# Two VectorE instructions of a graph dilation are tied to their place in the program

## The chip, the cores and the metric

The kernel runs on one NeuronCore of a Trainium2 chip. A core has TensorE (matmuls, here called PE), VectorE (DVE), ScalarE (ACT), GpSimd (POOL) and SyncE (SP, which here only issues transfers). The metric is the device time of one execution in microseconds; the figure given for a kernel is the median of its runs.

## The reference

Two graph layers follow each other on 16 graphs of 1024 nodes with 128 features each, in float32. Each layer normalises x, applies a relu, runs three convolutions and adds its result to x.

Layer 0 is, three times over for each graph:

```
h   = h @ W + b
nh  = h / |h|
ew  = adj * (nh @ nh.T)      # cosine of every pair of nodes times the edge
h   = ew @ h                 # relu after the first two
```

Layer 1 first thins out each graph's adjacency, which is the *dilation*. It goes through the rows one after the other, and each row's removals also clear the column:

```
row  = carry[n]; num = sum(row); sf = (num + 1) // 2 if num > 10 else 1
rank = cumsum(row)
rm   = row & (rank % sf == 0)          # if the node is valid and num > 1
carry[n] = row & ~rm;  carry[:, n] &= ~rm
```

Three graph convolutions with batch normalisation over all nodes follow on the thinned adjacency, then a projection. The result of the dilation depends on adj alone, so it can be worked out while layer 0 runs.

## The kernel before, in words

**Two strands.** The first part of the kernel interleaves layer 0 (the generator `layer0`) with the dilation (the generator `dilation`). The loop at the end of that part takes one step of the dilation, and then as many steps of layer 0 as bring both to the same share of their estimated work; the numbers that the generators yield are these estimates. This fixes only the order in which the program is written down.

**Who sets the order on an engine.** The program is written with a tile framework whose scheduler reorders each engine's instructions: it simulates the kernel and, among instructions whose inputs it takes as ready, issues first what was written first. So an instruction that is written late but ready early can be placed far ahead. `tc.keep_in_program_order(ins)` takes this freedom from one instruction: it puts an edge from the instruction that was written just before it on the same engine, so that it is issued behind that one. The edge concerns the order of issue alone; no semaphore is waited for. Two kinds of instructions of the dilation have such an edge before the change: the scans on VectorE (line 741) and the |rank - shift| on ScalarE (line 751).

**Layer 0.** The adjacency of a graph is brought in by blocks of 128 x 128. `adj_piece` (line 245) loads a block column into `nat` (two buffers), `adjT_tile` (line 253) loads the rows into `adjA`, and TensorE turns `nat` (line 260). For each block row, `products` multiplies the normalised features on TensorE into `pg` (line 344, two PSUM buffers), and VectorE multiplies `pg` with the adjacency into `ew` (lines 353 and 356). `turn` transposes ew (lines 373 and 374), and `sums` and `sums_back` add up ew @ h in PSUM (lines 384 and 398). Here as everywhere, an engine works through its queue in the order in which it was placed.

**The dilation.** Rows are treated in 8 blocks of 128, and each block in two halves of 8 graphs, which makes 16 half blocks. Each has three phases:

- *loads*, for each of the 8 graphs: the rows of adj come into `an` (line 585, two buffers). ScalarE turns the part from the diagonal on into a 0/1 pattern (lines 587 and 588: Sign, then Relu with a row sum, `rest`). For the part left of the diagonal, the columns removed by earlier blocks come through a transposing DMA from DRAM into `kl` (line 591, two buffers), and VectorE makes the pattern and its row sum `left` in one instruction, **line 594**. After every fourth graph, the diagonal blocks are turned and multiplied on TensorE (608 to 616) into the distances `T` (618), with `rbias` from VectorE (611).
- *rounds*: an iteration over the 128 rows of the block that finds which of them remove which diagonal entries (`Z`, `E`, `x`; lines 625 to 722).
- *scans*, for each of the 8 graphs: VectorE runs the cumulative sum over 1024 columns, `rank` (line 741). One graph later ScalarE takes |rank - shift| (line 751), and VectorE compares it with `radius`, **line 762**, which gives `kp`: 1 where an edge stays. GpSimd stores it to DRAM (line 763).

The loads of the next half block are written one by one between the scans of the present one: scan, layer-0 steps, load, layer-0 steps, comparison of the graph before, layer-0 steps, next scan. The patterns live in a ring of 10 slots, 8 for one half block and 2 ahead.

**After the dilation.** A flag tells whether an exact version has to run (a branch at line 824, not taken for these inputs). Layer 0 then ends, and layer 1 follows; none of it is edited.

Of the kernel before, what the change touches and what calls it, by code (L numbers as in the profile page):

```python
# [12 lines left out]
ALU = mybir.AluOpType  # L13
# [3 lines left out]
P = 128  # L17
# [29 lines left out]
def tile_adj_preln_d2(  # L47
# [40 lines left out]
    nc = tc.nc  # L88
# [111 lines left out]
    with ExitStack() as actx:  # L200
# [18 lines left out]
        for fill, value, op in ((0.0, -2.0, ALU.is_ge), (4.0 * FAR, 2.0 * FAR, ALU.is_gt)):  # L219
# [4 lines left out]
                up, up, pattern=[[1, P]], compare_op=op, fill=fill, base=0, channel_multiplier=-1  # L224
# [338 lines left out]
        def dilate(k, half, exact):  # L563
# [6 lines left out]
            def pattern(i):  # L570
                return patt[:, (at0 + i) % SLOTS, :]

            left = poold.tile([P, BH], F32, tag="left", name=f"left{nk}")
# [7 lines left out]
            def loads():  # L581
                for i in range(BH):
                    b = half * BH + i
                    an = poold.tile([P, N], F32, tag="an", name=f"an{nk}_{i}")
                    nc.sync.dma_start(an, adj[b, cols, :])
                    on = pattern(i)[:, 2 + k * P :]
                    nc.scalar.activation(on, an[:, k * P :], AF.Sign)
                    nc.scalar.activation(on, on, AF.Relu, accum_out=rest[:, i : i + 1])
                    if k:
                        pk = poold.tile([P, NCH - 1, P], F16, tag="kl", name=f"kl{nk}_{i}")  # L590
                        nc.sync.dma_start(
                            pk[:, :k, :].rearrange("p j q -> p (j q)"), keep_d[b][: k * P, cols], transpose=True
                        )
                        nc.vector.scalar_tensor_tensor(
                            pattern(i)[:, 2 : 2 + k * P],
                            an[:, : k * P],
                            0.0,
                            pk[:, :k, :].rearrange("p j q -> p (j q)"),
                            ALU.is_gt,
                            ALU.mult,  # L600
                            accum_out=left[:, i : i + 1],
                        )
                    if i % GT == GT - 1:
                        four = range(i - GT + 1, i + 1)
                        bs_ = slice(i - GT + 1, i + 1)
                        pdt = ps_sm.tile([P, GT, P], F16, tag="sm", name=f"pdt{nk}_{i}")
                        for n, ii in enumerate(four):
                            nc.tensor.transpose(pdt[:, n, :], pattern(ii)[:, diag], ident16)
                        dT = poold.tile([P, GT, P], F16, tag="dT", bufs=1, name=f"dT{nk}_{i}")
                        nc.scalar.activation(dT, pdt, AF.Copy)  # L610
                        nc.vector.tensor_scalar(rbias[:, bs_], rest[:, bs_], 2.0, -2.0, ALU.mult, ALU.add)
                        pT = ps_sm.tile([P, GT, P], F32, tag="sm", name=f"pT{nk}_{i}")
                        for n, ii in enumerate(four):
                            nc.tensor.matmul(pT[:, n, :], lhsT=dT[:, n, :], rhs=upto, start=True, stop=False)
                            nc.tensor.matmul(pT[:, n, :], lhsT=pattern(ii)[:, diag], rhs=off, start=False, stop=False)
                            nc.tensor.matmul(pT[:, n, :], lhsT=ident16, rhs=after, start=False, stop=True)
                        for n, ii in enumerate(four):
                            nc.scalar.activation(T[:, ii, :], pT[:, n, :], AF.Identity, bias=rbias[:, ii : ii + 1])
                    yield 0.8
# [105 lines left out]
            def scans():  # L725

                i = 0
                while i < BH:
                    at_ = (at0 + i) % SLOTS
                    n = min(BH - i, SLOTS - at_)  # L730
                    here = patt[:, at_ : at_ + n, diag]
                    nc.vector.tensor_tensor(here, here, E[:, i : i + n, :], ALU.subtract)
                    i += n
                ranks = {}
                for i in range(BH + 1):
                    if i < BH:

                        pt = pattern(i)
                        ranks[i] = rank = poold.tile([P, N], F16, tag="rank", bufs=3, name=f"rank{nk}_{i}")
                        tc.keep_in_program_order(  # L740
                            nc.vector.tensor_tensor_scan(rank, pt[:, 1 : N + 1], pt[:, 2:], 0.0, ALU.add, ALU.add)  # L741
                        )
                        yield True, 2.5
                    if i == 0:
                        continue

                    i -= 1
                    b = half * BH + i
                    pt, rank = pattern(i), ranks.pop(i)
                    tc.keep_in_program_order(  # L750
                        nc.scalar.activation(  # L751
                            rank, rank, AF.Abs, bias=shift[:, i : i + 1], scale=1.0 if exact else -1.0
                        )
                    )
                    kp = poold.tile([P, N], F16, tag="kp", name=f"kp{nk}_{i}")
                    if exact:
                        nc.vector.tensor_scalar(
                            kp, rank, low[:, i : i + 1], radius[:, i : i + 1], ALU.max, ALU.not_equal
                        )
                        nc.vector.tensor_tensor(kp, kp, pt[:, 2:], ALU.is_ge)  # L760
                    else:
                        nc.vector.tensor_scalar(kp, rank, radius[:, i : i + 1], None, ALU.not_equal)
                    nc.gpsimd.dma_start(keep_d[b][cols, :], kp)
                    yield False, 0.8

            return loads(), rounds(), scans()

        units0 = layer0()
# [448 lines left out]
```

## Time and profile before

| | |
|---|---|
| median of 3 runs | 2819.08 us (2816.39 to 2822.73) |
| the profiled execution | 2820.68 us |
| its span, first to last instruction | 2818.8 us |
| PE busy in the span | 2649.9 us, 94% |
| DVE busy | 1947.1 us, 69% |
| ACT busy | 1426.5 us, 51% |
| POOL busy | 477.6 us, 17% |
| scans, line 741 | 128, 2305 ns each |
| comparisons, line 762 | 128, 547 ns each |
| patterns left of the diagonal, line 594 | 112, 769 ns each |

The dilation lies in the first 1524 us of the span. In the waits of the profile, "PE pg L344 <- DVE ew L356" reads: the TensorE instruction of line 344 that writes pg waited for the VectorE instruction of line 356 that writes ew. Waits and idle times of an engine that is not the bound cost nothing by themselves. DVE_READ_ACCUMULATOR rows belong to the instruction ahead of them; it fetches a row sum.

### The profile page before, as it was taken

Reading aid. Unit: us, or ns where it says so; the run is one execution under the profiler, and the core shown is the slowest. Engines: PE = TensorE matmul, PEld = TensorE weight load, DVE = VectorE, ACT = ScalarE, POOL = GpSimd, SP = SyncE. Lnnn points to the kernel's source line nnn. Section 1 sums busy time; section 2 is a strip of 40 time slices with the busy share of each in tenths; the row PEclk is TensorE's granted clock in tenths of the full one; section 3 lists DMA queues with packets and bytes.
Section 4 is the critical chain, followed back from the end, with each engine's and each line's share of the span. In section 5 each row is a group of like instructions: output and inputs, shape, how many; then the busy total and the mean of one; then the engine's idle time right before and its main releaser. Section 6 shows DMA issues by size and latency. Waiting matters only on the chain. (4 is left out here: it accounts for less than half of the span.)

```text
span 2818.8 us, 51980 instructions
## 1 busy us (share of the span) xinstructions
PE 2649.9 (94%) x18803; PEld 2193.2 (78%) x18803; DVE 1947.1 (69%) x4943; ACT 1426.5 (51%) x4097; POOL 477.6 (17%) x616
## 2 busy tenths in 40 slices
PE   6999999999999999999999999999989999999997
PEld 4666666676776676666676778888889999899997
DVE  3778778788888788889886467777762333456556
ACT  6757667558556566466454333343333334333334
POOL 3112112012012111121121012222220101010101
PEclk9999999999999999999999999999999999999999
DMA  8437347258366476386354069999976666576774
GB/s 283 135 128 241 99 159 240 75 159 245 85 201 173 101 226 186 95 254 182 93 178 162 1 234 386 402 402 387 402 297 214 203 216 201 188 238 228 234 237 135
DMA packets 382233, 585.22 MB, mean 208 GB/s; under 512 B 85200, under 2 KB 266448, under 8 KB 381968
## 3 DMA queue, kind: packets, MB, share of 16 engines
q1 hardware_dynamic: 343280, 425.28, 48.2%
q0 software_dynamic: 38688, 156.53, 14.8%
q8 instruction: 151, 2.47, 0.4%
q14 instruction: 114, 0.93, 0.1%
HBM read 403.44 MB, written 163.58 MB: 201 GB/s over the span
## 5 line engine op out<-in xcount | busy, mean ns | idle before, releaser
L890 PE MATMUL agg<-hw,aT 128*128 128x128 f32 (+1 forms) x6144 | 743.5, 277 | 8.2 <-DVE aT L995 7.3
L890 PEld LDWEIGHTS agg<-hw,aT 128*128 128x128 f32 x6144 | 713.4, 193 | 13.6 <-DVE aT L995 9.7
L344 PE MATMUL pg<-nhT 128*128 128x512 f32 (+3 forms) x1152 | 454.7, 497 | 40.4 <-DVE ew L356 39.1
L384 PE MATMUL po<-ew,hS 128*128 128x512 f32 (+3 forms) x1152 | 453.3, 497 | 8.1 <-ACT hTo L407 3.7
L356 DVE TENSOR_TENSOR ew<-pg,adjA 128x768 f32<-128x768 f32 (+3 forms) x528 | 423.6, 826 | 5.0 <-PE pg L344 5.0
L398 PEld LDWEIGHTS po<-ew,hS 128*128 128x128 f32 x2688 | 339.5, 193 | 39.1 <-issue 36.8
L398 PE MATMUL po<-ew,hS 128*128 128x128 f32 x2688 | 367.5, 277 | 1.2 <-ACT ew L374 1.2
L374 ACT ACTIVATE ew<-gt 128x512 f32<-128x512 f32 (+1 forms) x480 | 208.5, 464 | 245.3 <-PE gt L373 238.0
L741 DVE TENSOR_TENSOR_SCAN rank<-patt 128x1024 f16<-128x1024 f16 x128 | 294.9, 2305 | 0.1
L344 PEld LDWEIGHTS pg<-nhT 128*128 128x128 f32 x1152 | 187.9, 192 | 131.7 <-issue 89.3
L384 PEld LDWEIGHTS po<-ew,hS 128*128 128x128 f32 x1152 | 195.2, 193 | 99.8 <-issue 64.6
L373 PEld LDWEIGHTS gt<-ident,ew 128*128 128x128 f32 x1344 | 168.5, 143 | 100.7 <-issue 75.4
L373 PE MATMUL gt<-ident,ew 128*128 128x128 f32 x1344 | 212.3, 277 | 4.8 <-PEq L824 2.5
L948 POOL TENSOR_TENSOR o<-o,rn 128x512 f32<-128x512 f32 x93 | 108.5, 1167 | 638.3 <-DVE rn L942 627.6
L353 DVE TENSOR_TENSOR ew<-pg,adjA 128x128 f32<-128x128 f32 x384 | 108.1, 282 | 156.6 <-PE pg L344 117.3
L864 DVE TENSOR_TENSOR own<-pw,bs 128x256 f32<-128x256 f32 x192 | 81.4, 424 | 155.5 <-ACT hw L863 155.4
L862 PE MATMUL pw<-wrx,hT 128*128 128x256 f32 x768 | 179.7, 388 | 9.2 <-ACT hT L1065 8.4
L862 PEld LDWEIGHTS pw<-wrx,hT 128*128 128x128 f32 x768 | 145.1, 194 | 31.3 <-ACT hT L1065 9.2
L1013 ACT ACTIVATE aT<-pta 128x512 f32<-128x512 f32 (+3 forms) x160 | 71.3, 467 | 187.4 <-PE pta L1012 181.9
L751 ACT ACTIVATE rank<-rank,fin 128x1024 f16<-128x1024 f16 x128 | 146.7, 1151 | 36.3 <-DVE rank L741 35.6
L940 ACT ACTIVATE own<-o 128x128 f32<-128x128 f32 x378 | 112.7, 301 | 99.7 <-DVE o L919 99.5
L321 POOL TENSOR_TENSOR hS<-hN,rn 128x1024 f32<-128x1024 f32 x48 | 102.5, 2136 | 355.5 <-DVE rn L157 226.0
(169 smaller groups left out, 3930.6 us busy)
## 6 DMA issues: line engine op xcount, KB each, us to landing
an<-in_adj_dram SPq DMA_DIRECT2D x128, 512.0 KB, 4.3
keep<-kp POOLq DMA_DIRECT2D x128, 256.0 KB, 2.9
kb<-keep SPq DMA_DIRECT2D x128, 256.0 KB, 5.5
aT<-adT SPq DMA_DIRECT2D x32, 960.0 KB, 4.7
aT<-adT SPq DMA_DIRECT2D x32, 832.0 KB, 4.6
aT<-adT SPq DMA_DIRECT2D x32, 704.0 KB, 4.2
aT<-adT SPq DMA_DIRECT2D x32, 576.0 KB, 3.4
xb<-in_x_dram SPq DMA_DIRECT2D x31, 512.0 KB, 5.2
```

Source lines behind the costliest of these rows:

```text
L344: nc.tensor.matmul(pg[:, :n, :].rearrange("p c q -> p (c q)"), lhsT=self.nhT[:, q * P : (q + 1) * P], rhs=self.nhT[:, (q + c) * P : (q + c ...
L356: nc.vector.tensor_tensor(both[0][:, :, off, :], pg[:, own:n, :].unsqueeze(1).to_broadcast([P, 2, n - own, P]), both[1][:, :, off, :], ALU ...
L373: nc.tensor.transpose(pt[:, i, :], ew[:, at + i, :], ident)
L374: nc.scalar.activation(ew[:, at : at + n, :], pt[:, :n, :], AF.Copy)
L384: nc.tensor.matmul(self.po[:, c * P : (c + n) * P], lhsT=self.hS[:, q, :], rhs=ew[:, c - q : c - q + n, :].rearrange("p c q -> p (c q)"), ...
L398: nc.tensor.matmul(self.po[:, q * P : (q + 1) * P], lhsT=self.hS[:, q + n, :], rhs=ew[:, NCH - 1 - q + n, :], start=False, stop=closes and ...
L741: nc.vector.tensor_tensor_scan(rank, pt[:, 1 : N + 1], pt[:, 2:], 0.0, ALU.add, ALU.add)
L751: nc.scalar.activation(rank, rank, AF.Abs, bias=shift[:, i : i + 1], scale=1.0 if exact else -1.0)
L862: nc.tensor.matmul(pw[:, i, :], lhsT=hT[:, 2 * h + i, :], rhs=wrx[:, l, :], start=True, stop=True)
L890: nc.tensor.matmul(self.place(c), lhsT=aT[:, blk, :], rhs=self.hw[:, source, :], start=source == 0 and c % self.ga == 0, stop=ends(c, source),
L940: nc.scalar.activation(sq, o, AF.Square, accum_out=ss[:, c : c + 1])
L948: nc.gpsimd.tensor_tensor(self.o[:, hc, :], self.o[:, hc, :], rn.unsqueeze(2).to_broadcast([P, CPH, D]), ALU.mult)
```

## The change

The instruction of line 594 (the pattern left of the diagonal) and that of line 762 (the comparison of the ranks) are each wrapped in `tc.keep_in_program_order`. What they compute is unchanged. The variant of the comparison that belongs to the exact version stays as it is. Lines behind the edits carry numbers that are up to two higher afterwards.

```diff
-                        nc.vector.scalar_tensor_tensor(
-                            pattern(i)[:, 2 : 2 + k * P],
-                            an[:, : k * P],
-                            0.0,
-                            pk[:, :k, :].rearrange("p j q -> p (j q)"),
-                            ALU.is_gt,
-                            ALU.mult,
-                            accum_out=left[:, i : i + 1],
+                        tc.keep_in_program_order(
+                            nc.vector.scalar_tensor_tensor(
+                                pattern(i)[:, 2 : 2 + k * P],
+                                an[:, : k * P],
+                                0.0,
+                                pk[:, :k, :].rearrange("p j q -> p (j q)"),
+                                ALU.is_gt,
+                                ALU.mult,
+                                accum_out=left[:, i : i + 1],
+                            )
                         )
...
                     else:
-                        nc.vector.tensor_scalar(kp, rank, radius[:, i : i + 1], None, ALU.not_equal)
+                        tc.keep_in_program_order(nc.vector.tensor_scalar(kp, rank, radius[:, i : i + 1], None, ALU.not_equal))
                     nc.gpsimd.dma_start(keep_d[b][cols, :], kp)
```

## The prediction

> **What bounds the kernel now.** I read the table of stretches first, then the waits of TensorE, then the timeline around the longest of them, then the waits of the DMA queue and the groups of the two edited lines. The branch of line 824 ends the only part in which the built programs differ: behind it every engine has the same instructions in the same order. So the stretch from 80 us (set-up) to 1524 us (branch) is the one to read; columns are start:end, length, then busy us and (count) by engine, TensorE clock, DMA share, GB/s.
>
> ```profile
> core 0: us, PE busy (x) PEld busy (x) DVE busy (x) ACT busy (x) POOL busy (x), PEclk, DMA share, GB/s
> 80.00:1524.00 1444.00, 1362.54 (x8627) 994.60 (x8626) 1194.50 (x2811) 896.55 (x2392) 251.94 (x314) 0.99 0.55 161
> ```
>
> TensorE is busy in 94% of it, VectorE in 83%. TensorE is the bound; VectorE matters only where TensorE waits for it. That is 1444 - 1362.5 = 81.5 us of idle TensorE at most, and these are its largest waits there:
>
> ```profile
> engine line waited for: us in total, times, longest us
> PE pg L344 <- DVE ew L356: 39.1, 37, 3.2
> PE pT L614 <- ACT dT L610: 5.5, 7, 1.4
> PE pw L293 <- ACT adjA L261: 4.2, 6, 0.9
> ```
>
> Half of the idle time is one wait: the cosine products pg have two PSUM buffers, and TensorE stands until VectorE has multiplied an older one into ew. What VectorE did instead is in the timeline before one such wait (start, length, engine, line; last a row of TensorE):
>
> ```profile
> 947.75 0.44 DVE L762 TENSOR_SCALAR kp<-rank,fin 128x1024 f16<-128x1024 f16 x1
> 948.10 2.29 DVE L741 TENSOR_TENSOR_SCAN rank<-patt 128x1024 f16<-128x1024 f16 x1
> 950.30 2.45 DVE L594 SCALAR_TENSOR_TENSOR patt<-an,kl 128x640 f16<-128x640 f32 x1
> ...
> 952.69 0.28 DVE L353 TENSOR_TENSOR ew<-pg,adjA 128x128 f32<-128x128 f32 x1
> 952.89 2.07 DVE L356 TENSOR_TENSOR ew<-pg,adjA 128x768 f32<-128x768 f32 x2
> ...
> 953.98 0.46 PE L344 MATMUL pg<-nhT 128*128 128x128 f32 x2 [2.86 <-DVE ew L356]
> ```
>
> A comparison, a scan and a pattern stand in one run of 4.9 us ahead of ew, and TensorE loses 2.86 us. Going through all 37 waits in this way, a pattern of line 594 lies in the run directly ahead in 22, which hold 26.6 of the 39.1 us.
>
> The two lines that are edited, as groups (busy us, mean ns | idle before them):
>
> ```profile
> L594 DVE SCALAR_TENSOR_TENSOR patt<-an,kl 128x128 f16<-128x128 f32 (+6 forms) x112 | 85.5, 769 | 6.8 <-DMA kl<-keep 5.9
> ...
> L762 DVE TENSOR_SCALAR kp<-rank,fin 128x1024 f16<-128x1024 f16 x128 | 69.2, 547 | 55.5 <-ACT rank L751 55.1
> ```
>
> VectorE idles 55.5 us in front of comparisons, since ScalarE's |rank - shift| is late, and hardly in front of patterns. The DMA queue's own waits:
>
> ```profile
> SPq L585 <- DVE patt L594: 397.9, 59, 48.6
> SPq L245 <- PE pt_a L260: 186.8, 81, 8.1
> ...
> SPq L253 <- DVE ew L356: 91.8, 42, 12.0
> ```
>
> The loads of adjacency rows (line 585) wait for the pattern two loads earlier to free their buffer.
>
> **What the Trainium skill says.** "PSUM — Partial Sum Buffer", section "Engine vs sequencer instructions": VectorE's and ScalarE's queues are strict first-in first-out. The trace agrees: ew at 952.69 follows the 2.45 us pattern. So an instruction queued too early costs what stands behind it. "Perfetto Trace Analysis", section "Identifying the Most-Contended Engine": improve that engine, and judge TensorE by LDWEIGHTS share rather than matmul share. That share here is 994.6/1444 = 69%, so busy TensorE may hide a little more than 81.5 us; I don't count on it. "SBUF — State Buffer", section "SBUF: two separate sides": VectorE and GpSimd lock a shared port pair for a whole instruction. The trace agrees: 8 patterns run over 0.2 us beyond their shape's median (2.45 against 0.82 us), and all 8 overlap a GpSimd multiply. The edit leaves such meetings to chance.
>
> **The change part by part.** Nothing is added or removed: both edits put an issue-order edge to the VectorE instruction traced just before, with no semaphore. What moves is where the scheduler places things, which the built orders show. Part of VectorE's queue in one half block (S scan, p pattern, k comparison, . the first ew product of a row):
>
> ```
> before  Sp..Sp..k.S.pk.S.p.kk.Sp..Sp..kSkSp..p..
> after   S.p.S.p.k.S.pk.S.p.k.S.pk.S.p.kS..pkS..p
> ```
>
> *Patterns.* All 112 move later, by 13.2 us of layer-0 VectorE work in the mean (24.5 us of the old trace's time in the median). They went in as soon as their data was expected; now one follows each scan, usually behind an ew row. Two estimates of the gain. Upper: take from each of the 22 waits the patterns ahead of it, min(wait, pattern): 20 us, or 20/86 = 0.23 us of TensorE per us of pattern. Lower: the patterns still run, and lengthen other runs. Adding up, at the trace's median durations, all that stands between ew products, what exceeds 3 us per run goes from 230 us to 195 us in the new order, 15% less, and runs above 4 us from 64 to 59; 15% of 39.1 us is 6 us. I take 9 us, nearer to the lower one because it counts what the patterns displace.
>
> *Comparisons.* Against layer-0 work, 88 of 128 stay within 0.5 us, 32 go later, 8 earlier, and of those with the largest waits (4.34, 3.88, 3.28, 3.10 us) none moves. They wait for ScalarE, whose |rank - shift| was pinned before. I cost this part at nothing, 0 to -3 us.
>
> *Loads.* Of each an the buffer is freed later, so an and kl fall 3.5 and 4.1 places back in the DMA queue among the layer-0 loads (one or two in the median), which go ahead; TensorE waits only 1.7 us for nat here, so little is gained. The kl loads (transposing, median 4.1 us to landing) ended 14.2 us ahead of their pattern in the median; placing the new order on the old trace's times leaves 12.5 us, 3.6 us at the least. So nothing waits; without that cover a pattern waiting for kl holds ew behind it, at 0.23 us of TensorE per us.
>
> *ScalarE.* Sign and Relu of the diagonal's right side (587, 588) move 2.8 us of ScalarE work later. They stood 93.5 us in ScalarE's queue waiting for a scan to free a pattern slot, with the transposed ew copies behind them. Part of that falls away; TensorE's waits on ScalarE are some 16 us, so I take -1 us (0 to -3). The later Relu leaves the diagonal transposes (608) about 10 of their 20 us, and rbias (611), 8.9 us later, at least 3.0 us before ScalarE needs it (before: 9.5 at the least from the second block on).
>
> *TensorE, GpSimd.* Of 5035 layer-0 TensorE rows 211 shift by over three places; keep stores move by at most two GpSimd places. Nothing.
>
> Sum: -9 - 0 - 1 - 0 = -10 us on a span of 2818.8 us, plus the 1.9 us around it: 2810.7 us, against 2820.68 us for the profiled execution. That one lay 1.6 us above the median of 2819.08 us, so the median becomes 2809 us.
>
> **The rivals.** *No measurable change, 2816 us.* The patterns only pass their delay to other ew rows, and waits on the scans (2.3 us each, most of every run) remain; about 3 us is left. For it: 15 of the 37 waits have no pattern ahead. Against it: the runs above 3 us do shrink. *A larger gain, 2797 us.* The upper estimate holds (20 us), with 2 us by ScalarE. For it: the new order has one pattern per scan, so that two patterns or scan plus pattern seldom meet. Against it: "pk" and "pkS" runs are new. *Slower, 2827 us.* The two-deep rings of an and kl lose their lead: a pattern, no longer early, finds kl not landed, as in three cases now (5.9 us, one of 2.87 us). At 0.23 us of TensorE per us, it takes (10 + 5.6)/0.23 = 68 us of VectorE waits at patterns, 0.6 us for each, to become measurably slower; 80 us of them give 18 - 10 = +8 us. For it: landings reach 8.8 us and the queue's other loads wait up to 12 us ahead of kl. Against it: the 12.5 us of lead.
>
> **How the numbers follow.** Some 0.2% (5.6 us) is what a measurement of this kernel can tell from no change. Likeliest case (6 to 15 us less) 0.44, larger gain 0.18, no change 0.20, slower 0.18: faster 0.62, same 0.20, slower 0.18. The range from 2796 (20 + 3 us) to 2826 us reaches into the slower case, which holds its upper edge; the likeliest case's own is 2804 to 2813 us.
>
> **What would show it.** In the profile after: pg waiting for ew (39.1 us) falls to about 30 us, the times from 37 to some 30; idle before comparisons stays near 50 us, which also shows that half of the edit idle; the wait of 585 for the pattern stays or grows, with no harm; idle before patterns stays under 15 us; Sign's wait for the scan falls below 93.5 us; from the branch on, lengths stay. I am wrong if idle before patterns or before Z (20.3 us now, on ScalarE's T) rises by tens of us, or if TensorE's waits for ew do not fall.

## The result, and the profile after

The changed kernel takes 2833.51 us (median; 2826.82 to 2838.3), against 2820.34 us of the kernel before (2816.39 to 2822.73) beside it: a ratio of 1.0045 with a 95% interval of 1.0025 to 1.0066. It is slower by 13 us, where 2809 us was forecast, and lies above the forecast range of 2796 to 2826 us. The second comparison, among the experiments, gave 1.0049 (1.0032 to 1.0065).

The stretch that differs, from 80 us to the branch, in the profile after (columns as in the prediction):

```profile
80.00:1528.00 1448.00, 1358.25 (x8615) 992.37 (x8616) 1191.65 (x2810) 890.99 (x2387) 248.28 (x314) 1.00 0.55 160
```

The branch comes 4 us later than before (1528 against 1524). TensorE is idle for 1448 - 1358.25 = 89.8 us, 8.3 us more, and busy for 4.3 us less (some 3.4 us of that are two stretches of half clock fewer, by the reckoning of the last section). Its waits in that stretch (engine, line and what it waited for; us in total, times, longest):

```profile
PE pg L344 <- DVE ew L356: 16.7, 26, 2.2
PE po L384 <- ACT hTo L407: 13.7, 15, 2.2
PE pw L293 <- ACT adjA L261: 7.7, 3, 3.7
PE pt_n L165 <- ACT adjA L261: 5.6, 6, 1.8
```

The wait for ew, half of the idle time before, fell from 39.1 to 16.7 us. In its place stand waits for ScalarE. The one for hTo was, before:

```profile
PE po L384 <- ACT hTo L407: 3.7, 6, 1.1
```

I put each idle gap of TensorE down to the engine that ended it:

| TensorE idle from 80 us to the branch, ended by | before | after |
|---|---|---|
| VectorE's ew (lines 353 and 356) | 40.9 | 19.9 |
| other VectorE | 14.1 | 17.0 |
| ScalarE | 20.8 | 48.6 |

So 21 us were won and 31 us lost. What holds ScalarE back is in its own waits after:

```profile
ACT patt L587 <- DMA an<-in_adj_dram: 171.4, 74, 5.5
...
ACT patt L587 <- DVE rank L743: 8.4, 5, 2.9
```

The same two waits before, when the scan's line had the number 741:

```profile
ACT patt L587 <- DVE rank L741: 93.5, 73, 2.9
...
ACT patt L587 <- DMA an<-in_adj_dram: 3.6, 3, 2.0
```

So Sign (line 587) waited for the scan to free a slot, and hardly for its load. Now it hardly waits for the scan, and 171 us for the load of an. The groups of the three lines, after (busy us, mean ns | idle before them, by what ended it; the whole kernel):

```profile
L587 ACT ACTIVATE patt<-an 128x1024 f16<-128x1024 f32 (+7 forms) x128 | 87.7, 686 | 189.4 <-DMA an<-in_adj_dram 180.8 <-DVE rank L743 8.4
L595 DVE SCALAR_TENSOR_TENSOR patt<-an,kl 128x128 f16<-128x128 f32 (+6 forms) x112 | 84.0, 750 | 0.1
L764 DVE TENSOR_SCALAR kp<-rank,fin 128x1024 f16<-128x1024 f16 x128 | 71.8, 563 | 55.6 <-ACT rank L753 55.4
```

VectorE's pattern, which reads the same load, waits for nothing: it comes so late that its data always lie there. That lateness is what the DMA queue sees:

```profile
SPq L585 <- DVE patt L595: 507.4, 85, 40.9
```

Line 585 loads an into a ring of two buffers, and a load starts when the pattern two graphs earlier has freed one. It stood 397.9 us for the pattern before, 507.4 us now. The timeline shows one case from end to end (start, length, engine, line; in brackets how long the engine stood idle, and for what):

```profile
831.57 0.68 DVE L595 SCALAR_TENSOR_TENSOR patt<-an,kl 128x512 f16<-128x512 f32 x1
832.32 1.05 SPq L585 DMA_DIRECT2D an<-in_adj_dram  x1
836.24 0.19 ACT L319 ACTIVATION_READ_ACCUMULATOR hS<-hN 128x1 f32 x1
840.01 0.63 ACT L587 ACTIVATE patt<-an 128x512 f16<-128x512 f32 x1 [3.58 <-DMA an<-in_adj_dram]
840.55 0.96 ACT L261 ACTIVATE adjA<-pt_a 128x512 f32<-128x512 f32 x2
841.18 1.16 PE L293 MATMUL pw<-w,hT 128*128 128x128 f32 x8 [3.63 <-ACT adjA L261]
```

The pattern ends at 832.25, which frees its buffer. The load that goes there is issued at once, but lands only at 840. ScalarE has been through with hS since 836.43 and has Sign next in its queue. It stands 3.58 us, and adjA, whose input TensorE had ready by 836.7, stands behind Sign. TensorE waits 3.63 us for adjA. That agrees with what the Trainium skill says on strict first-in first-out queues ("PSUM — Partial Sum Buffer", section "Engine vs sequencer instructions"); the prediction used it for VectorE and ew, and the same holds on ScalarE for adjA, hTo and the transposed ew.

The profile explains +6.1 us of its own execution (2826.82 against 2820.68): some 4 us up to the branch, some 2.5 behind it, where the two kernels do not differ. That execution is the shortest of the after kernel's first four. The other 7 us of the difference of the medians are taken up in the last section.

### The profile page after: what moved, and what is told of

Read it like the earlier page. It is cut to its first block, busy times and chain, and to the rows that moved or that the text cites. A ratio compares the mean times of both kernels' runs of the same rounds, so it can differ in the third digit from the quotient of the medians.

```text
span 2825.0 us, 51959 instructions
## 1 busy us (share of the span) xinstructions
PE 2643.9 (94%) x18803; PEld 2188.5 (77%) x18803; DVE 1944.9 (69%) x4943; ACT 1422.4 (50%) x4097; POOL 473.1 (17%) x616
## 5 line engine op out<-in xcount | busy, mean ns | idle before, releaser
L344 PE MATMUL pg<-nhT 128*128 128x512 f32 (+3 forms) x1152 | 453.8, 496 | 19.9 <-DVE ew L356 17.1
L398 PEld LDWEIGHTS po<-ew,hS 128*128 128x128 f32 x2688 | 338.1, 192 | 41.1 <-issue 38.6
L587 ACT ACTIVATE patt<-an 128x1024 f16<-128x1024 f32 (+7 forms) x128 | 87.7, 686 | 189.4 <-DMA an<-in_adj_dram 180.8
L765 POOL DMA_DIRECT2D keep<-kp x128 | 70.7, 553 | 534.8 <-DVE kp L764 463.0
```

The lines of the kernel that those rows point to most:

```text
L344: nc.tensor.matmul(pg[:, :n, :].rearrange("p c q -> p (c q)"), lhsT=self.nhT[:, q * P : (q + 1) * P], rhs=self.nhT[:, (q + c) * P : (q + c ...
L398: nc.tensor.matmul(self.po[:, q * P : (q + 1) * P], lhsT=self.hS[:, q + n, :], rhs=ew[:, NCH - 1 - q + n, :], start=False, stop=closes and ...
```

## The experiments

Two readers, ScalarE's Sign and VectorE's pattern, share each load of an. The theories: **A**, the late pattern frees the buffer late, so Sign waits for its load and blocks ScalarE; **B**, the edge on the comparison costs the time; **C**, any reshuffle of VectorE's queue moves the time, with no link to an. Each kernel is compared with the kernel before on its chip (medians 2817.58 to 2819.68 us).

| | what is tied | median us | ratio (95%) | ew wait | Sign's wait for an | pattern's wait for an |
|---|---|---|---|---|---|---|
| 1 | pattern | 2835.39 | 1.0067 (1.0050 to 1.0084) | 24.5 | 166.9 | 0 |
| 2 | comparison | 2804.82 | 0.9947 (0.9932 to 0.9963) | 25.8 | 0 | 0 |
| 3 | pattern, comparison, Sign | 2790.20 | 0.9899 (0.9883 to 0.9915) | 15.2 | 0.5 | 0 |
| 4 | as after, an three deep | 2849.62 | 1.0099 (1.0081 to 1.0117) | 19.5 | 127.8 | 0 |
| 5 | as after, an and kl three deep | 2811.22 | 0.9971 (0.9962 to 0.9981) | 13.9 | 60.5 | 0 |
| 6 | nothing, an one deep | 2849.81 | 1.0111 (1.0095 to 1.0126) | 38.7 | 61.6 | 29.6 |
| 7 | Sign | 2835.38 | 1.0061 (1.0048 to 1.0074) | 35.5 | 0 | 63.7 |
| 8 | comparison, Sign | 2834.23 | 1.0063 (1.0044 to 1.0083) | 33.4 | 0 | 66.4 |
| 9 | pattern, Sign | 2790.25 | 0.9901 (0.9886 to 0.9916) | 15.3 | 0.5 | 0 |
| 10 | as after, again | 2831.24 | 1.0049 (1.0032 to 1.0065) | 15.2 | 161.4 | 0 |

Waits are in us, from 80 us to the branch, each from one profiled execution. The ew wait is that of line 344 for line 356.

**1 and 2: each half of the change alone.** Of the diff, only its first part, and only its second, in short:

```diff
+                        tc.keep_in_program_order(
                             nc.vector.scalar_tensor_tensor(
                                 pattern(i)[:, 2 : 2 + k * P],
...
+                        tc.keep_in_program_order(nc.vector.tensor_scalar(kp, rank, radius[:, i : i + 1], None, ALU.not_equal))
```

> The pattern of line 594 alone is tied; the comparison is as before. Theory A (ScalarE's Sign now stands for the adjacency load an, because the late pattern frees the load's buffer late; TensorE pays through ScalarE's later copies): as the changed kernel, 2826 to 2838 us, ScalarE waits for an 140 to 200 us in all (11 to 15 us in the kernel before), TensorE waits for ew 12 to 25 us. Theory B (the tied comparisons hold up VectorE and so cost the time): 2797 to 2812 us, since only the useful half is left. Theory C (any shuffle of the order moves the time by some tenths of a per cent, whatever waits change): anything from 2808 to 2838 us, without relation to the wait for an.

> The comparison of line 762 alone is tied; the pattern is as before. Theory A: as the kernel before within 5 us (2815 to 2825 us), ScalarE waits for an below 30 us, TensorE waits for ew near 39 us. Theory B: slower, 2826 to 2838 us. Theory C: 2808 to 2838 us.

The pattern's edge alone gives the whole loss, 17 us, as A expected, and ScalarE's waits show the same picture:

```profile
ACT patt L587 <- DMA an<-in_adj_dram: 166.9, 73, 6.2
```

The comparison's edge alone makes the kernel faster by 13 to 15 us, which no theory expected. B falls. TensorE's wait for ew in that kernel:

```profile
PE pg L344 <- DVE ew L356: 25.8, 34, 3.2
```

Only some 20 comparisons and the scans behind them move, by up to 11.3 us of VectorE's layer-0 work. Yet seven of the largest ew waits (1.45 to 2.86 us, 14.7 us together, the 2.86 us at 954 us that the prediction shows among them) are gone; others go up a little. Sign waits for the scan much as before (103.3 us) and TensorE's idle time for ScalarE is unchanged (20.2 us, 20.8 before). So this half acts through VectorE's runs: TensorE's idle time up to the branch falls from 81.5 to 69.6 us.

**3: the other reader tied as well.** The changed kernel, and in line 587:

```diff
-                    nc.scalar.activation(on, an[:, k * P :], AF.Sign)
+                    tc.keep_in_program_order(nc.scalar.activation(on, an[:, k * P :], AF.Sign))
```

> The changed kernel, with ScalarE's Sign (line 587) tied to its place in the program too, so that it is queued about one scan's distance behind the load instead of directly behind it. Theory A: ScalarE waits for an fall from 171 us to below 40 us, TensorE's waits on ScalarE (hTo, adjA, hT; 33 us in the changed kernel) to 20 us or less, waits for ew stay at 12 to 25 us, and the time is 2797 to 2814 us, faster than the kernel before. Theory B: 2826 to 2838 us, as the comparisons are still tied. Theory C: 2808 to 2838 us.

It takes 28 us off the kernel before and 41 to 43 off the changed one, a little more than A expected. The stretch to the branch, and ScalarE's wait for an in it:

```profile
80.00:1491.00 1411.00, 1355.00 (x8622) 988.36 (x8621) 1191.73 (x2811) 898.24 (x2393) 249.95 (x314) 1.00 0.56 165
```

```profile
ACT patt L587 <- DMA an<-in_adj_dram: 0.5, 1, 0.5
```

The branch comes at 1491 us, 37 us earlier than after. TensorE's idle time is 1411 - 1355 = 56 us, 34 less than after, and of that ScalarE ends 11.9 us instead of 48.6. The gain of the late pattern stays: TensorE's wait for ew is 15.2 us. A single edge on ScalarE, on a line that the change leaves alone, turns the loss into a gain. The time lies below the range of C, and C has no account of it.

**4 and 5: a deeper ring instead.** In 4, a third buffer for an; to find room, the tiles T and Z have one buffer instead of two. In 5, also a third for kl, and E has one buffer too.

```diff
-                    an = poold.tile([P, N], F32, tag="an", name=f"an{nk}_{i}")
+                    an = poold.tile([P, N], F32, tag="an", bufs=3, name=f"an{nk}_{i}")
...
-                        pk = poold.tile([P, NCH - 1, P], F16, tag="kl", name=f"kl{nk}_{i}")
+                        pk = poold.tile([P, NCH - 1, P], F16, tag="kl", bufs=3, name=f"kl{nk}_{i}")
```

The second part is in 5 alone.

> The changed kernel with three buffers for an instead of two (T and Z have one buffer instead of two to make room; each is dead before its next writer). The load then no longer waits for the pattern two graphs back, but three. Theory A: ScalarE waits for an below 60 us, time 2797 to 2816 us. Theory B: 2826 to 2838 us. Theory C: 2808 to 2838 us.

> The changed kernel with three buffers for an and three for kl (E, T and Z have one each to make room). With three an alone the next an still stood behind a kl that waits for the pattern two graphs back, in the same transfer queue. Theory A (ScalarE stands for an, and that is what the tied pattern costs): ScalarE waits for an fall from 171 us to below 50 us, those of Sign for the scan come back to 60 to 100 us as in the kernel before, waits for ew stay at 12 to 25 us, time 2800 to 2816 us. Theory C (any shuffle moves the time, whatever the waits): no relation to the wait, 2805 to 2850 us.

4 missed: it is slower than the changed kernel and than all three theories allowed, and Sign still waits 127.8 us. The waits of ScalarE and of the DMA queue in 4:

```profile
ACT patt L587 <- DMA an<-in_adj_dram: 127.8, 45, 5.6
...
SPq L591 <- DVE patt L595: 192.1, 22, 40.8
```

Line 591 loads kl, into a ring that the same pattern frees and that is still two deep. It stands in the same queue ahead of the next an, so the next load of an often stands behind a kl that waits for the pattern, though its own buffer is free (line 585 waits for no pattern any more). That says why Sign's wait fell no further; it does not say why 4 is some 15 us slower than the changed kernel. With both rings three deep (5), that is relieved, by ScalarE's waits:

```profile
ACT patt L587 <- DVE rank L743: 66.7, 41, 3.2
ACT patt L587 <- DMA an<-in_adj_dram: 60.5, 29, 4.7
```

Part of Sign's waiting has gone back to the scan, as it was before the change, and the kernel is faster than before. The time is as A expected; Sign's wait was to fall further (below 50 us). What the single buffers of T, Z and E cost in 4 and 5 was not run apart, so neither size belongs to the rings alone.

**6: the opposite, with nothing tied.** In the kernel before:

```diff
-                    an = poold.tile([P, N], F32, tag="an", name=f"an{nk}_{i}")
+                    an = poold.tile([P, N], F32, tag="an", bufs=1, name=f"an{nk}_{i}")
```

> The kernel before, nothing tied, with one buffer for an instead of two: each load waits until Sign and pattern of the graph before have both run. Theory A: ScalarE waits for an rise from 13 us to 100 us or more, and the time by 8 to 30 us, to 2828 to 2850 us, with waits for ew near 39 us and more of TensorE's waits on ScalarE. Theory C: no relation to that wait.

Without any edge a shorter ring costs some 30 us, as A expected. The waits for an, of ScalarE and of VectorE:

```profile
ACT patt L587 <- DMA an<-in_adj_dram: 61.6, 29, 7.1
...
DVE patt L594 <- DMA an<-in_adj_dram: 29.6, 21, 4.0
```

A expected 100 us or more for Sign alone; here both readers share the wait.

**7 and 8: Sign tied, the pattern free.** The edit of line 587 that 3 has, in the kernel before; in 8 the comparison's edge as well.

> The kernel before with ScalarE's Sign alone tied to its place; pattern and comparison as before. Theory A (waits at the head of ScalarE's queue cost time, for the load or for the scan alike): Sign's waits for the scan, 93.5 us, fall below 40 us, and the time to 2798 to 2812 us, less gain than with all three tied since the runs ahead of ew stay. If instead the pattern's edge was needed for the gain of the kernel with all three tied: 2815 to 2823 us.

> Comparison and Sign tied, the pattern left free. If the two edges' gains add (13 us for the comparison, 5 to 15 us for Sign), 2790 to 2800 us, and the pattern's edge is then worth nothing; if the pattern's edge gives its share once Sign is out of the way, this kernel is 5 to 12 us slower than the one with all three tied (2795 to 2804 us).

Both are slower than A expected, and they complete the mechanism. VectorE's wait and the DMA queue's in 7:

```profile
DVE patt L594 <- DMA an<-in_adj_dram: 63.7, 35, 5.3
...
SPq L585 <- ACT patt L587: 320.0, 76, 22.9
```

and in 8:

```profile
DVE patt L594 <- DMA an<-in_adj_dram: 66.4, 37, 4.5
```

With Sign late, it is Sign that frees the buffer late (line 585 stood 37.5 us for it before), and now the pattern, still placed early, stands at the head of VectorE's queue with layer 0's products behind it. TensorE does not pay for this at ew, whose wait even falls a little, but at VectorE's other results; the largest in 7 (3.7, 2.8 and 1.9 us before):

```profile
PE pc L673 <- DVE E L667: 9.2, 7, 3.8
PE pt_h L165 <- DVE x L421: 6.4, 7, 2.5
PE pt_a L260 <- DVE hN L297: 5.6, 4, 3.2
```

By engine, TensorE's idle time for VectorE other than ew goes from 14.1 us to 32.6 us in 7 and 30.3 us in 8, while that for ScalarE falls from 20.8 to some 15 us. The loss is as large as the change's own. It does not come from the pattern being late as such, but from one reader being late while the other is early.

**9: both readers tied, the comparison free.** The changed kernel with the edge of line 587 and without that of the comparison.

> Pattern and Sign tied, the two readers of an, and the comparison free. The theory now: of two readers of a two-deep ring, a tied one frees the load late and the free one then stands for it at the head of its queue, so the pair has to be tied together; the comparison's edge is a separate gain. Then ScalarE's Sign and VectorE's pattern both wait less than 15 us for an, and the time lies below the kernel before, 2796 to 2812 us, slower than the kernel with all three tied by 5 to 15 us. If the comparison's edge were what makes the kernel with all three tied fast, this one is at 2815 us or above.

Neither reader waits for an (0.5 us and nothing), as expected. The time equals that of kernel 3 within 0.1 us (ratios 0.9901 and 0.9899), where 5 to 15 us more were expected. So the comparison's gain in 2 does not add: what it removed is already gone once both readers are tied (the ew wait is 15.3 us here, 15.2 in 3). In 8, it bought nothing either.

**10: the changed kernel again.**

> The changed kernel once more, for its time on one chip with more runs: 2826 to 2838 us by the first measurement, ScalarE waits for an 150 to 190 us.

Both expectations hold. Its executions spread from 2813.54 to 2836.53 us, wider than the kernel before beside it (2813.28 to 2823.34).

How long after its issue a load of an is used says the same in one table. Loads and readers are paired in order, in the traces, from 80 us to the branch (median us from the issue of line 585 to the reader's start):

| | to Sign | to the pattern |
|---|---|---|
| before | 17.0 | 17.5 |
| after | 4.9 | 18.7 |
| 3, all three tied | 15.9 | 17.1 |
| 7, Sign tied | 19.3 | 5.7 |

In the same stretch of these four traces a load lands 4.0 to 4.2 us after its issue in the median, and 8.5 us at the latest. Where one reader follows at 4.9 or 5.7 us, it stands waiting for the slower landings; where both follow at some 16 us or more, next to none is waited for (3.6 us before, 0.5 us in 3). That the scheduler places the untied reader as soon as it takes the load for landed is my reading of these numbers; they show where it was placed, not why.

## Why the prediction was wrong

- **Loads**, "so nothing waits": this step failed. It asked whether kl would be there in time for the pattern on VectorE, and it was: idle before patterns is 0.1 us. It did not ask the same for an and its other reader. The step even noted that each an buffer is freed later, and then costed only the queue of the loads. The time from the issue of a load to Sign fell from 17.0 to 4.9 us, and ScalarE stood 171.4 us for these loads instead of 3.6.
- **ScalarE**, -1 us: failed with it. Sign's wait for the scan fell as said, from 93.5 to 8.4 us, but only because Sign now stands for its load first. Both waits together went from 97 to 180 us, and TensorE's idle time for ScalarE from 20.8 to 48.6 us: +28 where -1 was entered (from some 16 us, which was low too). I had taken the scan's wait as a cost that goes; it was a wait that gives way to the next one.
- **Patterns**, -9 us: the mechanism was right and the size low. With the pattern alone tied (kernel 1) TensorE's wait for ew is 24.5 us, 15 us less, between the two estimates of 6 and 20 us. In the changed kernel it is 16.7 us in 26 waits (about 30 forecast); the other 8 us come with the comparison's edge. That the lower estimate went by the length of runs, and not by which of them TensorE stood behind, is a likely reason for its size, but was not tried.
- **Comparisons**, nothing: wrong alone, by 14 us (kernel 2), though idle before comparisons stayed at 55.6 us as forecast. Counting how many move, and that those with the largest own waits stay, does not say which ew rows stood behind the some 20 that move later. Beside both other edges it is worth nothing (3 against 9). On top of the pattern's edge it takes 7 us off TensorE's idle time for ew (27.2 to 19.9 us), but the idle time for ScalarE is 7.5 us longer (41.1 to 48.6); the medians differ by some 3 us (2831 to 2834 in 10 and after, 2835 in 1), less than these intervals resolve.
- The part behind the branch was to keep its length, and does within 2.5 us. **TensorE, GpSimd**, nothing: no wait in the traces speaks against it, but it was not tried apart.
- The slower **rival** had the sign and the wrong place. It let a two-deep ring lose its lead, at kl and on VectorE, where there were 12.5 us of lead. The ring that lost it was an's, on ScalarE, where only 3.6 us of waiting stood in the waits of before, and the lead was never worked out.
- The **signs of being wrong** that it named stayed away: idle before patterns is 0.1 us, idle before Z fell from 20.3 to 12.6 us, and TensorE's waits for ew fell. None of them concerned what ScalarE's Sign waits for.

In its own terms the sum would have been -21 (ew, by patterns and comparisons together) + 28 (ScalarE) + 3 (other VectorE) - 1 (the rest) = +9 us of TensorE idle time, against 8.3 us measured.

## What to carry to other kernels

When a load has several readers in a shallow ring, an edge on one of them moves the landing of a later load, which every other reader waits for: work out the lead of each reader on each engine, and do not tie one without the others. Here one reader alone cost 13 to 17 us, on either engine, and both together took off 27 to 28 us. A wait that is cut short in an in-order queue is a gain only if nothing else becomes last there; look for the next releaser before booking it. And once the place is known, the remedy can be one line on the other engine: kernel 3 (or 9, with one edge less) is faster than both kernels of this case.

## What the runs showed of the hardware

TensorE's granted clock drops to about half for stretches of 3.4 us (once in some traces, of twice that), and most of them begin close to the end of one of its longer waits. The kernel before, around the 2.86 us wait at 954 us (three stretches; columns as in the prediction, of which the clock, the DMA share and GB/s are the last):

```profile
951.00:955.00 4.00, 1.14 (x7) 0.74 (x6) 4.00 (x6) 1.98 (x5) 1.61 (x2) 0.97 0.44 137
955.00:958.40 3.40, 3.40 (x15) 2.65 (x14) 1.62 (x8) 1.09 (x2) 0.00 (x0) 0.54 0.97 198
958.40:962.00 3.60, 3.60 (x19) 2.35 (x18) 2.02 (x3) 0.08 (x1) 0.00 (x0) 1.00 0.76 121
```

TensorE is busy for all of the second stretch, but at a clock of 0.54. Seven 128-column transposes of line 373 take 1.70 us in it, and 0.93 us at full clock elsewhere. By that, such a stretch costs some 3.4/2 = 1.7 us, an estimate. From 80 us to the branch the trace of before has six, at six of its seven largest waits, all for ew (1.90 to 3.18 us; one of 1.91 us has none). The trace after has four, at its four largest waits, all for ScalarE (2.60 to 3.72 us); waits of 2.16 and 2.21 us have none. Kernel 2 has two, kernels 3 and 9, whose longest wait is 1.75 us, none. So a long wait can cost more than itself, which neither the prediction's 0.23 us per us nor its sums held. Length alone does not decide: in kernel 10 a wait of 2.72 us has none, and one of 1.23 us has one. The Trainium skill describes the gate ("TensorE: Matmul & The Clock Gate", section "HAM oscillation — how this bites in real kernels") and names idle gaps above about 3.4 us as what trips it; here all six of before followed shorter waits, of 1.90 to 3.18 us. Which length, and what else around it, trips the gate was not tried apart.

This also bears on the 7 us of the medians that the profile after does not show. Over all executions of the changed kernel, the mean granted clock goes from 0.990 in the shortest (2813.54 us) to 0.984 in the longest (2838.3 us). 0.006 of 2830 us is 17 us, of the 25 us between them. The profiled execution had 0.988, the other three of the first comparison 0.984 and 0.985. At 0.003 less clock they would be 8.5 us longer, about what is missing. This is rough: the profiled execution of before had 0.985, lower than most others of its kernel, and is still close to their median; and the mean clock counts the set-up too, where half-clock stretches cost 0 to 14 us of clock time in these traces without an edit there. The trace of kernel 10, which is that of its shortest execution, fits: two half-clock stretches instead of four (3.4 us), 84.6 us of idle TensorE instead of 90, and the branch at 1518 us. For the long executions the share of the clock is argued and not shown: there is no trace of them.
